# Attention 3 of a four-layer model: search for the largest scores in pairs and by chunks of keys, preparation in steps over more PSUM banks

## The chip, the cores and the metric

The kernel runs as one program on one core of a Trainium2 chip. The metric is the device time in microseconds (us), the median of several runs. Five engines matter: PE (TensorE, matrix products and transposes, which write to PSUM), DVE (VectorE), ACT (ScalarE), POOL (GpSimd) and the DMA queues, which have nothing to do in the stage that is edited. PSUM has eight banks; each bank here holds one tile of 512 float32 columns.

## The reference, cut to what matters

The input is an image pair `x` of shape (2, 56, 56, 128). Layers 0 and 1 are state-space blocks, layer 2 is an attention and a spectral mixer, layer 3 an attention and a layer of experts. The edited code belongs to the two attentions, above all the one of layer 3, over L = 3136 tokens of each of two images:

```python
def _L3_attn_ref(x, Wq, bq, Wk, bk, Wv, bv):
    TEMP = (2 * 128) ** 0.5
    q = jnp.einsum('bnf,of->bno', x, Wq) + bq
    k = jnp.einsum('bnf,of->bno', x, Wk) + bk
    v = jnp.einsum('bnf,of->bno', x, Wv) + bv
    scores = jnp.einsum('bnf,bmf->bnm', q, k) / TEMP
    alpha = jax.nn.softmax(scores, axis=-1)
    out = jnp.einsum('bnm,bmf->bnf', alpha, v)
    return out
...
t = _to_tokens(x)
t = t + _L2_attn_ref(_ln_t(t))
t = t + _L2_ffn_ref(_ln_t(t), L2_ffn_sigma, L2_ffn_phi, L2_ffn_M_u, L2_ffn_M_phi_plus, L2_ffn_M_phi_minus, L2_ffn_log_weights, L2_ffn_gumbel)
t = t + _L3_attn_ref(_ln_t(t), L3_attn_Wq, L3_attn_bq, L3_attn_Wk, L3_attn_bk, L3_attn_Wv, L3_attn_bv)
t = t + _L3_ffn_ref(_ln_t(t), L3_ffn_gate_w, L3_ffn_gate_b, L3_ffn_weight1, L3_ffn_weight2)
```

Layer 2's attention (`_L2_attn_ref`) is the same without projections: queries, keys and values are the normalised tokens, and a token doesn't attend to itself.

## The kernel before

The kernel does the layers one after the other. Layer 2's attention is `Attention2`, then comes the mixer, then layer 3's attention, `Attention3`, then the experts. Both attentions run the class `Attend`.

**Attend.run** goes over 14 chunks of queries: two images (`b`) with seven chunks (`qc`) of 448 tokens each. A chunk goes in 25 steps `j` over tiles of 128 keys (the last has 64). In a step PE makes the scores of the key tile against the 448 queries (L1031, into a bank `sc`), ACT takes the exponential into a tile `e` (L1033), POOL adds `e` to `total` (L1042, L1044), and PE adds the product of the values with `e` to the accumulator `acc`, in a bank `av` (L1025). This last product lags by two steps. At the end of the chunk DVE copies `acc` to `by` (L1055), PE multiplies it with the output weights (L1059, into `pt`) and sums `total` over keys with a column of ones (L1062, into `pd`, a second tile of the pool `av`), DVE takes the reciprocal (L1066) and adds the scaled result to the tokens `X` (L1069). A float32 product of 448 columns is two instructions in the trace.

**Queries** is for layer 3 alone. The exponential needs a shift, an estimate of the largest score of each query. `begin` makes the queries of a chunk (L949, bank `lo`), adds a bias on ACT (L953) and casts them to bfloat16 (L955). `some(left)` then works off a list of 28 search tiles: four groups `i` of 112 queries by seven chunks `c` of keys. Each is one bfloat16 product (L966, into the bank `lo`, of which there is one) and one maximum on DVE (L971). The list has `i` outside and `c` inside; after the seventh tile of a group, the maximum of the seven maxima is taken (L973) and turned into a row by PE (L974, into a bank `pr` that is held over the whole search). After the fourth group ACT copies the row (L980), PE spreads it over 128 partitions (L982) and DVE adds it to the queries (L983), which the scores of the chunk wait for. While a chunk is worked on, the next chunk's search is issued step by step, so that after step `j` at most `28 * (21 - j) // 21` tiles are left.

**Attention3.run** first prepares the seven chunks of image 0, with `chunk`: it adds the mixer's result `A`, turned by PE (L1180), to the tokens (L1181), normalises them (`layernorm_tokens`: L77 to L83 on DVE, with a square and a square root on ACT, L80 and L82, and a product on POOL, L84), turns them into channels (L1189), evacuates these to `uT`, casts a bfloat16 copy `low` on POOL (L1192) and turns key tiles into values (`key_tiles`, L1202). All banks of a chunk come from `sc`. The chunks of image 1 are prepared by the function `then`, at the end of the query chunks of image 0, with the bank `pt`: one at the end of each of the chunks 0 to 4, and two at the end of chunk 5.

PSUM in `Attend` is divided into three banks `sc`, two `av`, and one each of `lo`, `pr` and `pt`.

The order in which an engine gets its instructions is made by the framework when the program is built, from the order in the source, the dependencies and the buffers; in the trace the first query (L949) stands between the second and third preparation, although the source issues it after the seventh. At run time an engine follows its fixed order.

Of the kernel before, what the change touches and what calls it, by code (L numbers as in the profile page):

```python
# [14 lines left out]
F32 = mybir.dt.float32  # L15
BF16 = mybir.dt.bfloat16
# [103 lines left out]
class Scans:  # L120
# [177 lines left out]
    def run(self):  # L298
        with ExitStack() as ctx:
            self.open(ctx)  # L300
            with self.k.tc.manual_schedule():
                self.all_steps()
# [622 lines left out]
def four(ps):  # L925

    return ps[:TP].rearrange("p (i c) -> p i c", c=C)


class Queries:  # L930
# [13 lines left out]
    def begin(self, b, qc):  # L944
        nc = self.k.nc
        self.b = b
        self.todo = [(i, c) for i in range(4) for c in range(NCH)]
        ps = self.banks("lo")
        nc.tensor.matmul(  # L949
            ps[:, 0:CH], lhsT=self.weights, rhs=self.keys[b][:, CH * qc : CH * (qc + 1)], start=True, stop=True  # L950
        )
        self.q = self.sp.tile([128, CH], F32, name="q")
        nc.scalar.activation(self.q, ps[:, 0:CH], AF.Identity, bias=self.bias)  # L953
        self.q16 = self.sp.tile([128, CH], BF16, name="q16")
        nc.vector.tensor_copy(self.q16, self.q)  # L955
        self.rows = self.banks("pr")

    def some(self, left):

        nc = self.k.nc  # L960
        while len(self.todo) > left:
            i, c = self.todo.pop(0)
            if c == 0:
                self.m = self.sp.tile([TP, NCH + 1], F32, name="m")
            ps = self.banks("lo")[:TP, 0:CH]
            nc.tensor.matmul(  # L966
                ps, lhsT=self.q16[:, TP * i : TP * (i + 1)], rhs=self.low[self.b][:, CH * c : CH * (c + 1)],
                start=True, stop=True,
            )
            m = self.m  # L970
            nc.vector.tensor_reduce(m[:, c : c + 1], ps, AX.X, ALU.max)  # L971
            if c == NCH - 1:
                nc.vector.tensor_reduce(m[:, NCH : NCH + 1], m[:, 0:NCH], AX.X, ALU.max, negate=True)  # L973
                nc.tensor.matmul(  # L974
                    self.rows[0:1, TP * i : TP * (i + 1)], lhsT=m[:, NCH : NCH + 1],
                    rhs=self.k.ident[:TP, :TP], start=True, stop=True,
                )
                if i == 3:
                    row = self.sp.tile([1, CH], BF16, name="shift")
                    nc.scalar.copy(row, self.rows[0:1, 0:CH])  # L980
                    ps = self.banks("pr")[:, 0:CH]
                    nc.tensor.matmul(ps, lhsT=self.part, rhs=row, start=True, stop=True)  # L982
                    nc.vector.tensor_tensor(self.q, self.q, ps, ALU.add)  # L983

    def take(self):
        self.some(0)
# [3 lines left out]
class Attend:  # L990
# [6 lines left out]
    def __init__(self, k, ctx):  # L997
        self.k = k
        self.sp = ctx.enter_context(k.pool("att", 6))
        self.ep = ctx.enter_context(k.pool("atts", 2))  # L1000
        pools = {"sc": 3, "av": 2, "lo": 1, "pr": 1, "pt": 1}
        self.pools = {n: ctx.enter_context(k.pool("p" + n, m, psum=True)) for n, m in pools.items()}
        self.ones = self.ep.tile([KT, 1], F32, name="onecol")
        k.nc.gpsimd.memset(self.ones, 1.0)
# [1 line left out]
    def bank(self, name):  # L1006
        return bank(self.pools[name], name)

    def run(self, keys, queries, V, scale, out_w, skip=None, then=lambda b, qc: None):

        k, nc, X = self.k, self.k.nc, self.k.X
        made = isinstance(queries, Queries)
        chunks = [(b, qc) for b in range(B) for qc in range(NCH)]
        if made:
            queries.begin(*chunks[0])
        for at, (b, qc) in enumerate(chunks):
            if made:
                q = queries.take()
            else:
                q = queries[b][:, CH * qc : CH * (qc + 1)]  # L1020
            acc = self.bank("av")[:, 0:CH]
            total = self.ep.tile([KT, CH], F32, name="total")

            def weigh(j, n, e):
                nc.tensor.matmul(acc, lhsT=V[b][:n, j, :], rhs=e[:n], start=j == 0, stop=j == NKT - 1)  # L1025

            waiting, first = [], None
            for j in range(NKT):
                n = min(KT, L - KT * j)
                ps = self.bank("sc")[:, 0:CH]  # L1030
                nc.tensor.matmul(ps[:n], lhsT=keys[b][:, KT * j : KT * j + n], rhs=q, start=True, stop=True)  # L1031
                e = self.sp.tile([KT, CH], F32, name="e")
                nc.scalar.activation(e[:n], ps[:n], AF.Exp, scale=scale)  # L1033
                if skip is not None:
                    c0, c1 = max(KT * j, CH * qc), min(KT * j + n, CH * (qc + 1))
                    if c0 < c1:
                        own = e[:n, c0 - CH * qc : c1 - CH * qc]
                        nc.vector.tensor_tensor(own, own, skip[:n, c0 - KT * j : c1 - KT * j], ALU.mult)  # L1038
                if j == 0:
                    first = e  # L1040
                elif j == 1:
                    nc.gpsimd.tensor_tensor(total, first, e, ALU.add)  # L1042
                else:
                    nc.gpsimd.tensor_tensor(total[:n], total[:n], e[:n], ALU.add)  # L1044
                if made and at + 1 < len(chunks):
                    if j == 0:
                        queries.begin(*chunks[at + 1])
                    queries.some(max(0, 28 * (21 - j) // 21))
                waiting.append((j, n, e))
                if len(waiting) > 2:  # L1050
                    weigh(*waiting.pop(0))
            for one in waiting:
                weigh(*one)
            by = self.ep.tile([128, CH], F32, name="by")
            nc.vector.tensor_copy(by, acc)  # L1055
            pt = four(self.bank("pt"))
            pd = self.bank("av")
            for i in range(4):
                nc.tensor.matmul(  # L1059
                    pt[:, i, :], lhsT=by[:, TP * i : TP * (i + 1)], rhs=out_w, start=True, stop=True  # L1060
                )
                nc.tensor.matmul(  # L1062
                    pd[:TP, i : i + 1], lhsT=total[:, TP * i : TP * (i + 1)], rhs=self.ones, start=True, stop=True
                )
            r = self.ep.tile([TP, 4], F32, name="r")
            nc.vector.reciprocal(r, pd[:TP, 0:4])  # L1066
            for i in range(4):
                xo = X[:, 4 * qc + i, b, :]
                nc.vector.scalar_tensor_tensor(xo, pt[:, i, :], r[:, i : i + 1], xo, ALU.mult, ALU.add)  # L1069
            then(b, qc)  # L1070


class Attention2:
# [40 lines left out]
class Attention3:  # L1114
# [35 lines left out]
    def run(self, A):  # L1150

        k = self.k
        with ExitStack() as ctx:
            kp = ctx.enter_context(k.pool("a3"))
            self.uT = [kp.tile([128, L], F32, name=f"u{b}") for b in range(B)]
            self.low = [kp.tile([128, L], BF16, name=f"low{b}") for b in range(B)]
            self.V = [kp.tile([KT, NKT, C], F32, name=f"V{b}") for b in range(B)]
            self.sp = ctx.enter_context(k.pool("a3u", 2))
            att = Attend(k, ctx)
            for c in range(NCH):  # L1160
                self.chunk(att, A, 0, c, "sc")

            def then(b, qc):

                if b == 0:
                    for c in {5: (5, 6), 6: ()}.get(qc, (qc,)):
                        self.chunk(att, A, 1, c, "pt")

            queries = Queries(k, self.uT, self.low, self.weights, self.c, att.ep, att.bank)
            att.run(self.uT, queries, self.V, 1.0 / 16, self.Wv, then=then)  # L1170

    def chunk(self, att, A, b, c, name):


        k, nc = self.k, self.k.nc
        x = k.X[:, 4 * c : 4 * (c + 1), b, :]
        ps = four(att.bank(name))
        for i in range(4):
            t = TP * (4 * c + i)
            nc.tensor.transpose(ps[:, i, :], A[:, b, t : t + TP], k.ident)  # L1180
# [3 lines left out]
        st = self.sp.tile([TP, 2, 4], F32, name="st")  # L1184
        layernorm_tokens(k, U, x, sq, st, C)
        nc.gpsimd.tensor_tensor(x, x, self.bias.unsqueeze(1).to_broadcast([TP, 4, C]), ALU.add)
        pt = att.bank(name)[:, 0:CH]
        for i in range(4):
            nc.tensor.transpose(pt[:, TP * i : TP * (i + 1)], U[:, i, :], k.ident[:TP, :TP])  # L1189
        uT = self.uT[b]  # L1190
        k.evacuate(uT[:, CH * c : CH * (c + 1)], pt, more=True)
        nc.gpsimd.tensor_copy(self.low[b][:, CH * c : CH * (c + 1)], uT[:, CH * c : CH * (c + 1)])  # L1192
        key_tiles(k, att.bank(name), uT, self.V[b], c)


def key_tiles(k, ps, uT, V, c):
# [679 lines left out]
```

## Time and profile before

| | |
|---|---|
| Time before | 9507.8 us, median of 3 runs (9499.12 to 9516.37) |
| The profiled execution's own time | 9515.81 us |
| Its span | 9513.7 us |
| PE busy in the span | 8186.0 us (86%) |
| Mean granted PE clock | 0.941 |
| Attention 2's chunks | 6081 to 6641 us |
| Attention 3, from its first transposes to its last accumulator | 8438.3 to 9271.9 us |
| Experts | 9274 to 9513.7 us |

The distances between the `by` copies (L1055), which end the accumulation of a chunk, show the pace of the chunks. In Attention 2 all are 40.0 us apart. In Attention 3 the first scores start at 8538.6, the first copy at 8584.6, and the distances are 52.0, 52.1, 52.0, 52.1, 52.0, 53.6 (image 0), 60.6, 52.3, 53.4, 55.2, 52.0, 54.8 and 45.1 us (image 1; in the last chunk no search follows).

How to read the profile: times are in us from the start of the span. A line of the timeline has the start, the duration, engine, source line, operation, the tiles it writes and reads, their shapes and a count; in brackets stand the idle time of the engine before it and what ended it. `PEld` is the load of weights into PE, which can run beside a product. The granted clock is the share of full speed that PE was given.

### The profile page before, as it was taken

What the parts mean: (1) busy time and instruction counts of PE and PEld (TensorE: products, weight loads), DVE (VectorE), ACT (ScalarE), POOL (GpSimd) and SP (SyncE); (2) the same over time, 40 slices, a digit from 0 to 9 for tenths busy, and PEclk for the clock granted to TensorE, in tenths of its full rate; (3) what the DMA queues carried; (4) which work ended last, traced back from release to release, by engine and by line L of the source; (5) the groups of instructions that cost most, each with busy time, mean ns of one, the idle gap of its engine ahead of it and who ended that gap; (6) DMA issues with size and microseconds to landing.
All of it is one profiled execution on the core that took longest, in us unless ns stands there. A gap on an engine that the chain in (4) does not pass through costs nothing. (4 is left out here: it accounts for less than half of the span.)

```text
span 9513.7 us, 94170 instructions
## 1 busy us (share of the span) xinstructions
PE 8186.0 (86%) x28803; PEld 4810.7 (51%) x28803; DVE 7093.3 (75%) x7484; ACT 3823.2 (40%) x6517; POOL 6321.7 (66%) x4006
## 2 busy tenths in 40 slices
PE   7888888888888888888888888699799999979997
PEld 3444444444444434444444444454688888854445
DVE  8999998999987997997998898401566766654433
ACT  4555545555445555555555555233111111113321
POOL 5999987999986996996997899666111111115550
PEclk9999999999999998998999999799899999979998
DMA  5766664666655884884885787000333333300005
GB/s 158 221 220 214 212 193 149 221 222 214 213 175 133 220 214 122 222 215 120 221 218 155 191 218 202 6 1 4 97 106 95 109 97 102 102 14 1 1 4 153
DMA packets 800676, 1367.59 MB, mean 144 GB/s; under 512 B 125373, under 2 KB 434366, under 8 KB 800138
## 3 DMA queue, kind: packets, MB, share of 16 engines
q1 hardware_dynamic: 800170, 1361.57, 50.2%
q8 instruction: 228, 3.74, 0.2%
q14 instruction: 278, 2.28, 0.1%
HBM read 1320.14 MB, written 41.11 MB: 143 GB/s over the span
## 5 line engine op out<-in xcount | busy, mean ns | idle before, releaser
L423 POOL TENSOR_TENSOR p<-h,c 128x784 f32<-128x784 f32 x2048 | 3762.5, 1860 | 238.9 <-PE acc L371 159.0
L371 PE MATMUL acc<-p,ident 128*128 128x392 f32 x8192 | 3138.5, 514 | 87.6 <-POOL p L423 86.0
L351 DVE TENSOR_TENSOR_SCAN h<-a,state,h 128x784 f32<-128x784 f32 x1536 | 2798.2, 1841 | 92.3 <-ACT a L332 70.4
L371 PEld LDWEIGHTS acc<-p,ident 128*128 128x128 f32 x8192 | 1523.6, 198 | 1178.6 <-POOL p L423 199.4
L410 DVE TENSOR_TENSOR h<-du,b 128x784 f32<-128x784 f32 x1408 | 1335.7, 949 | 182.5 <-PE b L357 178.5
L332 ACT ACTIVATE a<-delta,L0A 128x784 f32<-128x784 f32 x1024 | 938.8, 918 | 838.2 <-DVE h L351 836.4
L426 POOL TENSOR_TENSOR h<-du,b 128x784 f32<-128x784 f32 x640 | 1188.2, 1857 | 3.1 <-DMA b<-rows 3.1
L357 PE MATMUL b<-three,sel 96*128 96x512 bf16 (+1 forms) x2816 | 711.0, 334 | 551.7 <-DVE h L410 502.7
L332 ACT ACTIVATE a<-delta,L1A 128x784 f32<-128x784 f32 x1024 | 936.5, 917 | 535.5 <-DVE h L351 533.3
L351 DVE TENSOR_TENSOR_SCAN h<-a,h 128x784 f32<-128x784 f32 x512 | 901.9, 1780 | 39.8 <-ACT a L332 21.4
L1044 POOL TENSOR_TENSOR total<-total,e 128x448 f32<-128x448 f32 (+1 forms) x644 | 727.5, 1130 | 293.6 <-ACT e L1033 266.4
L1425 POOL TENSOR_TENSOR u<-u,S 128x1024 f32<-128x1024 f32 x64 | 150.0, 2365 | 1136.5 <-DVE S L1394 1136.5
L1394 DVE TENSOR_TENSOR u<-u,cv 128x512 f32<-128x512 f32 x1024 | 623.4, 681 | 342.7 <-PE cv L1381 341.3
L357 PEld LDWEIGHTS <-sel 96*128 96x128 bf16 x2816 | 276.0, 98 | 1163.8 <-issue 920.3
L1033 ACT ACTIVATE e<-sc 128x448 f32<-128x448 f32 (+1 forms) x700 | 379.7, 543 | 775.2 <-PE sc L1031 748.4
L971 DVE TENSOR_REDUCE m<-lo 112x1 f32<-112x448 f32 x392 | 244.7, 624 | 371.3 <-PE lo L966 370.0
L1396 ACT COPY u<-cv 128x512 f32<-128x512 f32 x256 | 149.3, 586 | 850.9 <-PE cv L1381 776.6
L1566 PE MATMUL pj<-u,Wm 128*128 128x196 f32 (+8 forms) x1536 | 354.5, 384 | 5.7 <-DVE A L1572 5.7
L1031 PE MATMUL sc<-q,u 128*128 128x448 f32 (+1 forms) x700 | 334.2, 566 | 7.3 <-DVE q L983 7.3
L1031 PE MATMUL sc<-big 128*128 128x448 f32 (+1 forms) x700 | 322.3, 546 | 12.4 <-ACT e L1033 12.4
L385 PE MATMUL acc<-big,ident 128*128 128x392 f32 x384 | 250.5, 784 | 92.4 <-ACT big L391 92.3
L1025 PE MATMUL av<-e,big 128*128 128x448 f32 (+1 forms) x700 | 320.6, 545 | 1.2 <-DVE e L1038 1.2
(394 smaller groups left out, 10527.4 us busy)
## 6 DMA issues: line engine op xcount, KB each, us to landing
c<-rows SPq DMA_DIRECT2D x1024, 392.0 KB, 4.0
c<-rows SPq DMA_DIRECT2D x2048, 196.0 KB, 4.4
b<-rows SPq DMA_DIRECT2D x320, 392.0 KB, 4.6
b<-rows SPq DMA_DIRECT2D x640, 196.0 KB, 4.5
H<-raw SPq DMA_DIRECT2D x32, 1568.0 KB, 7.0
wC<-win SPq DMA_DIRECT2D x64, 576.0 KB, 5.7
wA<-win SPq DMA_DIRECT2D x64, 384.0 KB, 5.4
wD<-win SPq DMA_DIRECT2D x64, 320.0 KB, 4.4
```

The source lines that it names most:

```text
L332: self.k.nc.scalar.activation(x["a"], g["delta"][ci], AF.Exp, scale=self.w["A"](g["kd"], ci, x["n"]))
L351: self.k.nc.vector.tensor_tensor_scan(h, a, h, start, ALU.mult, ALU.add)
L357: self.k.nc.tensor.matmul(ps[:, c0:c1], lhsT=self.w["selB"](x["n"]), rhs=x["g"]["three"][:, c0:c1], start=True, stop=True)
L371: nc.tensor.matmul(job["acc"][:, i, 0:392], lhsT=self.k.ident, rhs=x["p"][:, 392 * i : 392 * (i + 1)], start=False, stop=n == NS - 1,)
L410: nc.vector.tensor_tensor(one["h"], one["g"]["du"][one["ci"]], one["b"], ALU.mult)
L423: nc.gpsimd.tensor_tensor(now["p"], now["h"], now["c"], ALU.mult)
L426: nc.gpsimd.tensor_tensor(three["h"], three["g"]["du"][three["ci"]], three["b"], ALU.mult)
L1031: nc.tensor.matmul(ps[:n], lhsT=keys[b][:, KT * j : KT * j + n], rhs=q, start=True, stop=True)
L1033: nc.scalar.activation(e[:n], ps[:n], AF.Exp, scale=scale)
L1044: nc.gpsimd.tensor_tensor(total[:n], total[:n], e[:n], ALU.add)
L1394: nc.vector.tensor_tensor(place(o), place(o), ps, ALU.add)
L1566: nc.tensor.matmul(ps[:, lo - c0 : hi - c0], lhsT=Ws[f][:, eo, r, :], rhs=u[:, b, f, lo - a0 : hi - a0], start=f == 0, stop=f == 1,)
```

## The change

The diff touches both classes and the preparation:

- The list of search tiles has the chunks of keys outside and the groups of queries inside. The maxima of all tiles are kept in one tile `m`; when the list is empty one instruction takes the maximum of the seven for all four groups, and the four turns into a row follow one another.
- `lo` has two banks, `pt` is gone. The output product uses `pr`, and the row and its spread take banks `pr` only at the end of the search. `pd` becomes four columns of the bank of `acc`.
- In the chunks, after step `j` at most `30 - 2j` tiles are left.
- In the preparation `chunk` is split into `tokens`, `channels` and the existing `key_tiles`. For image 0, the tokens of the next chunk are issued ahead of the channels of this one, with banks `av` for the tokens and `sc` for the rest; the first query is made after the first chunk's channels, and four search tiles follow each chunk.
- Image 1 is prepared within the query chunks 0 to 3, two chunks in each of the first three and one in the fourth, by `also`, which is called in every step: tokens in step 1, channels in step 6, key tiles in step 9, and the same twelve steps later. All use the bank `pr`.

```diff
-        self.todo = [(i, c) for i in range(4) for c in range(NCH)]
+        self.todo = [(c, i) for c in range(NCH) for i in range(4)]
...
-        self.rows = self.banks("pr")
+        self.m = self.sp.tile([TP, 4, NCH], F32, name="m")
...
+            nc.vector.tensor_reduce(self.m[:, i, c : c + 1], ps, AX.X, ALU.max)
+        if not self.todo:
+            m = self.sp.tile([TP, 4], F32, name="mm")
+            nc.vector.tensor_reduce(m, self.m, AX.X, ALU.max, negate=True)
+            ps = self.banks("pr")
+            for i in range(4):
                 nc.tensor.matmul(
-                    self.rows[0:1, TP * i : TP * (i + 1)], lhsT=m[:, NCH : NCH + 1],
-                    rhs=self.k.ident[:TP, :TP], start=True, stop=True,
+                    ps[0:1, TP * i : TP * (i + 1)], lhsT=m[:, i : i + 1], rhs=self.k.ident[:TP, :TP],
+                    start=True, stop=True,
                 )
...
-        pools = {"sc": 3, "av": 2, "lo": 1, "pr": 1, "pt": 1}
+        pools = {"sc": 3, "av": 2, "lo": 2, "pr": 1}
...
-                    queries.some(max(0, 28 * (21 - j) // 21))
+                    queries.some(max(0, 30 - 2 * j))
                 waiting.append((j, n, e))
                 if len(waiting) > 2:
                     weigh(*waiting.pop(0))
+                also(at, j)
...
-            pt = four(self.bank("pt"))
-            pd = self.bank("av")
+            pt = four(self.bank("pr"))
+            pd = av[:TP, CH : CH + 4]
...
-            then(b, qc)
...
-                self.chunk(att, A, 0, c, "sc")
-
-            def then(b, qc):
-
-                if b == 0:
-                    for c in {5: (5, 6), 6: ()}.get(qc, (qc,)):
-                        self.chunk(att, A, 1, c, "pt")
...
+            U = {0: self.tokens(att.bank("av"), A, 0, 0)}
             for c in range(NCH):
+                if c + 1 < NCH:
+                    U[c + 1] = self.tokens(att.bank("av"), A, 0, c + 1)
+                self.channels(att.bank("sc"), U.pop(c), 0, c)
+                if c == 0:
+                    queries.begin(0, 0)
+                key_tiles(k, att.bank("sc"), self.uT[0], self.V[0], c)
+                queries.some(4 * (NCH - 1 - c))
+
+            def also(at, j):
+
+                half, part = divmod(j, 12)
+                c = 2 * at + half
+                if half > 1 or c >= NCH:
+                    return
+                if part == 1:
+                    U[c] = self.tokens(att.bank("pr"), A, 1, c)
+                elif part == 6:
+                    self.channels(att.bank("pr"), U.pop(c), 1, c)
+                elif part == 9:
+                    key_tiles(k, att.bank("pr"), self.uT[1], self.V[1], c)
+
+            att.run(self.uT, queries, self.V, 1.0 / 16, self.Wv, also=also)
```

`tokens` is the first half of `chunk` up to the bias on the tokens, and `channels` the second half up to the bfloat16 copy; their instructions are unchanged.

## The prediction

> **What bounds the kernel now.** I read the page first (TensorE, PE, busy 86% of the span), then the sums over windows for the stages that the edited code runs in, then the timeline inside them. The page's chain of waits was no help: it ends in the experts after this stage. The windows, from Attention 2 to the end (columns: stretch, length, busy time and count of PE, weight loads, DVE, ACT, POOL, then granted PE clock, DMA share, GB/s):
>
> ```profile
> 6081.00:6641.00 560.00, 558.03 (x1608) 281.52 (x1608) 43.10 (x135) 191.68 (x354) 380.16 (x342) 1.00 0.01 3
> 8438.30:8506.00 67.70, 23.85 (x95) 16.75 (x95) 29.95 (x59) 10.31 (x21) 20.01 (x21) 0.56 0.00 0
> 8506.00:8538.60 32.60, 17.32 (x38) 5.09 (x35) 16.03 (x30) 2.80 (x4) 0.00 (x0) 0.50 0.00 0
> 8538.60:8898.40 359.80, 346.58 (x1136) 176.44 (x1135) 161.93 (x312) 128.17 (x223) 208.74 (x189) 0.99 0.00 1
> 8898.40:9271.90 373.50, 353.68 (x1059) 174.77 (x1060) 134.47 (x260) 101.74 (x188) 189.79 (x168) 0.94 0.00 1
> ```
>
> Attention 2 (first row) runs its 14 chunks in 40.0 us each with PE always busy: the price of a chunk without search. Attention 3 has three parts: preparation of image 0 (67.7 us, no engine busy for half of it, PE clock 0.56), the rest of the first search (32.6 us), and the chunks, 733.3 us for 14, so 52.4 each. What is late in the second part is one bank, seen in the timeline:
>
> ```profile
> 8518.09 0.62 DVE L971 TENSOR_REDUCE m<-lo 112x1 f32<-112x448 f32 x1 [0.62 <-PE lo L966]
> 8518.76 0.53 PE L966 MATMUL lo<-low,q 128*112 128x448 bf16 x1 [0.71 <-DVE m L971]
> 8518.77 0.17 PEld L966 LDWEIGHTS <-q 128*112 128x112 bf16 x1 [1.07 <-issue]
> 8519.33 0.62 DVE L971 TENSOR_REDUCE m<-lo 112x1 f32<-112x448 f32 x1 [0.62 <-PE lo L966]
> 8520.01 0.53 PE L966 MATMUL lo<-low,q 128*112 128x448 bf16 x1 [0.71 <-DVE m L971]
> ```
>
> PE and DVE take turns: one tile of the search every 1.25 us, of which DVE works 0.62. The same happens between chunks, where the rest of the search stands before the next chunk's scores:
>
> ```profile
> 9121.80 0.38 PE L1059 MATMUL pt<-L3Wv,by 128*112 128x128 f32 x2
> 9122.68 1.02 PE L949 MATMUL lo<-u,M 128*128 128x448 f32 x2 [0.50 <-DVE m L971]
> 9123.63 0.35 PE L974 MATMUL pr<-ident,m 112*1 112x112 f32 x2
> 9124.83 0.34 PE L982 MATMUL pr<-shift,part 1*128 1x448 bf16 x1 [0.84 <-ACT shift L980]
> 9126.24 3.32 PE L1031 MATMUL sc<-q,u 128*128 128x448 f32 x4 [1.06 <-DVE q L983]
> ```
>
> From 9121.8 to 9126.2 PE has about 1.5 us of work; the rest is waiting for the chain maximum, transpose, copy, spread, add. And the preparation is one chain per chunk of tokens:
>
> ```profile
> 8454.81 1.01 PE L1189 MATMUL sc<-ident,U 112*128 112x112 f32 x4 [3.45 <-POOL U L84]
> 8456.53 1.11 PE L1202 MATMUL sc<-ident,u 128*128 128x128 f32 x4 [0.72 <-DVE u L62]
> 8457.44 1.06 PE L1180 MATMUL sc<-ident,A 128*112 128x128 f32 x4
> 8458.29 0.58 PE L966 MATMUL lo<-low,q 128*112 128x448 bf16 x1
> 8464.59 1.01 PE L1189 MATMUL sc<-ident,U 112*128 112x112 f32 x4 [5.71 <-POOL U L84]
> ```
>
> L1189 to L1189 is 9.8 us; the next chunk's first transposes (L1180) start only behind L1202, so two chains hardly overlap.
>
> **What the Trainium skill says.** TensorE: Matmul & The Clock Gate, Part 1 (What's actually happening): an array that has been idle runs at half clock, and some 3.4 us of sustained work release it. The trace agrees: granted clock 0.50 in the lone search, 1.00 in Attention 2, 0.94 for image 1's chunks. Trace Analysis (Optimizing Tensor Performance, Matmuls) advises rotating independent groups through PSUM banks so that evacuation overlaps the next group; the 1.25 us rhythm shows the want of it. PSUM — Partial Sum Buffer (PSUM bank collisions raise a hardware error): a bank must not be written by PE while DVE reads another part of it. No run here shows it, but it bears on an edit below: the denominators `pd` move into the bank that the copy `by` reads, so they should wait for that copy.
>
> **The change part by part.**
>
> *Preparation of image 0.* The same instructions in another order: tokens of c+1 stand before channels of c, in other banks, and four search tiles follow each chunk (chunk-outer order needs only the keys of that chunk). The chain from L1180 to the end of L84 is 7.1 us (8457.44 to 8464.54), and with two in flight it no longer sets the pace. DVE then does: per chunk 0.69+0.68+0.17+0.69+0.69+0.18 for the normalisation and 0.62 for the evacuation, 3.7 us, times 7 is 26.0; 28 reductions of 0.625 are 17.5; the cast of q 0.4. That is 44 us in 78 instructions; with about 0.06 us between two of them, 49. Ahead of DVE lie 0.8 us of transposes, about 4 us of idle DVE while only the first chains run, and behind it the chain to the first scores: after the last reduction before it took 4.9 us (8533.7 to 8538.6), 2.4 of which were the next query's L949; I take 4, and 4 for unlucky order. Sum 62 instead of 100.3: **gain 38** (28 if the pace is 8.3 us a chunk, 45 if DVE has no gaps). The table of ACT isn't concerned: no Exp runs there yet.
>
> *Search inside the chunks, two banks, two tiles a step.* What PE must do in a chunk: 40.0 (Attention 2's row), 28 search tiles at 0.19 (step between their starts in the loop) 5.3, L949 0.95, four L974 at 0.28 1.1, L982 0.2: 47.55. Preparing one chunk of image 1 adds 3 x 0.45 = 1.35 us. Chunks 1 to 5 do all this today in 52.0, so 48.9 is work and 3.1 waiting; image 1's chunks take 52.0 to 60.6 (54.8 in the mean) for 47.55 of work, because nothing is there to fill the waits and the clock falls to half for 3.4 to 13.7 us each time. With the budget 30-2j the last tile is issued at step 15 of 25, so the chain to q has nine steps (some 17 us) and ends before the chunk does; then the next scores can follow without a gap, as in Attention 2. Two tiles in a step cost DVE 2 x 0.625 plus gaps, 1.35 us, in a step of 1.5+0.38 = 1.88 us of PE: it fits, with 0.5 us to spare.
> The `by` copy is 0.62 us; the eight L1062 that ran beside it must now wait, and the next scores fill the place (three `sc` banks). Cost nothing; without that cover 0.7 x 28 = 20 us over both attentions.
> After, chunk by chunk, from first scores to the last `by`: chunk 0 46.0 + 2.7 (two preparations) + 2.6 (three more tiles and the chain) = 51.3; chunks 1 and 2 50.25; chunk 3 48.9; chunks 4 to 12 9 x 47.55 = 428; chunk 13 40.3. Sum 669, against 733: 64.
>
> *Image 1's preparation in three steps inside chunks 0 to 3.* Its PE work is in the sum. Its Sqrt takes ACT from the Exp table and back: 2 x 1.28 us of table loads, seven times before and after (ScalarE: Activation LUTs, What ACT_TABLE_LOAD costs, gives the same 1283 ns), so ACT is away for some 3.5 us while weighting lags scores by two steps (3.4 us). Its DVE operations (3.7 us) come into steps where the search uses 1.35 of 1.88. From the three steps of PE, the second stands 5 steps (9.4 us) behind the first; that chain took 8.9 us in chunk 2 before (8640.5 to 8649.4) and stalled PE 0.48. POOL has 27.1 us of sums in a chunk, plus 5.7 for two preparations: room enough. I charge 1 us for each of seven: 7 (between 0 and 21). **Gain of the chunks 57** (between 43 and 64).
>
> *Attention 2* uses the same class: its `pt` becomes `pr`, one bank as before, and `pd` as above: 0. The experts behind start earlier and are unchanged.
>
> Sum: 38 + 57 = 95 us of the profiled execution's 9515.8 (span 9513.7), which gives 9421. The median shown is 9507.8, 8 lower, within the 17 us by which its runs differ; against it the forecast is **9413**.
>
> **The rivals.**
> - *The loop keeps its waits* (9460). PE follows a fixed order, and if reductions and normalisation crowd DVE in chunks 0 to 3, or the chain to q is ordered late, the loop gains only some 10 us and preparation 38. For it: 0.5 us of slack in a step against DVE operations of 0.69. Against: in chunks 4 to 12 DVE has nothing else.
> - *More than that* (9385): preparation at 6 us a chunk (7 more) and an interior free of stalls (7), and PE warm before the first scores, with the chain to q hidden in part (14). For it: the clock gate's price is in all of today's gaps.
> - *Slower: the pair holds PE* (9606). If the second tile of a pair, in the fixed order, has to wait until the first is reduced, as with one bank, each step grows from 1.88 to 1.5+0.19+1.25 = 2.94 us: 1.06 us in 14 steps of 13 chunks, 193 us, less the 95. It decides from 0.52 us a pair (95 / 182). For it: DVE's in-order queue, busy 72% in these steps. Against: two banks free one after the other, and the second reduction ends about 1.7 us after the pair began, before its bank is wanted again at 2.07.
> - *Nothing happens* (9500): the order on the engines is made by the framework, which already pulled the first query's L949 ahead of the second chunk's end; it might undo the written order. Against: the banks, which bound it, do change.
>
> **How the numbers follow.** Likeliest 0.70 (its own range 9385 to 9440, from the bounds 28 to 45 and 43 to 64), loop keeps its waits 0.13, more 0.05, slower 0.08, nothing 0.04. The range 9378 to 9470 leaves out the last two and some tails. A measurement here tells 0.2% (19 us) from no change: faster 0.86, same 0.05, slower 0.09.
>
> **What would show it.** Right: first scores about 62 us after the first L1180; `by` copies 47.5 apart for chunks 4 to 12 with clock 1.00; no DVE wait ahead of the first scores of a chunk. Wrong: search matmuls in the loop that wait for `m` by 0.5 us or more; L1189 waiting for U by several us; `by` copies of Attention 2 no longer 40.0 apart.

## The result, and the profile after

The median went from 9509.49 us to **9401.65 us** (four runs each, 9499.12 to 9516.37 and 9399.84 to 9417.94): ratio 0.9891, 95% interval 0.9874 to 0.9908. The prediction knew three of the four runs before, with a median of 9507.8; its forecast was 9413 us with a range of 9378 to 9470. The profiled execution took 9399.84 us, span 9398.0.

The same sums over windows, of the changed kernel; the columns are those of the first view of the prediction. The rows are image 0's preparation, chunk 2 of the queries, chunks 4 to 12 together, and the last chunk:

```profile
8424.00:8482.00 58.00, 38.64 (x132) 20.91 (x131) 42.92 (x87) 12.65 (x25) 20.88 (x21) 0.56 0.00 1
...
8582.00:8634.10 52.10, 50.51 (x179) 26.73 (x179) 26.87 (x51) 22.92 (x37) 32.89 (x30) 1.00 0.00 0
...
8684.50:9112.70 428.20, 428.20 (x1396) 222.66 (x1396) 177.77 (x337) 132.87 (x243) 244.51 (x216) 1.00 0.00 1
9112.70:9152.70 40.00, 40.00 (x117) 20.16 (x116) 1.93 (x6) 13.61 (x25) 27.18 (x24) 1.00 0.00 1
```

From chunk 4 on PE is busy for 428.20 of 428.20 us at full clock: nine chunks at 47.6 us. The preparation with the first search, 100.3 us before, takes 57.9. The clock there is still 0.56; in a second profile of the changed kernel it was 0.62, for the same 57.9 us: that difference of the clock didn't change the length of the stage.

The seam between two chunks, in the timeline of PE (before, the seam shown in the prediction had waits of 0.50, 0.84 and 1.06 us):

```profile
8683.46 1.02 PE L1025 MATMUL av<-e,V 64*128 64x448 f32 x2
8684.41 1.02 PE L1031 MATMUL sc<-q,u 128*128 128x448 f32 x2
8685.26 0.92 PE L949 MATMUL lo<-u,M 128*128 128x448 f32 x2
8686.01 0.38 PE L1060 MATMUL pr<-L3Wv,by 128*112 128x128 f32 x2
8686.23 0.27 PE L1063 MATMUL av<-onecol,total 128*112 128x1 f32 x2
...
8687.60 1.75 PE L1031 MATMUL sc<-q,u 128*128 128x448 f32 x4
8689.19 0.54 PE L966 MATMUL lo<-low,q 128*112 128x448 bf16 x2
8689.57 0.92 PE L1025 MATMUL av<-e,V 128*128 128x448 f32 x2
```

No line has a bracket, so PE waits for nothing. The next chunk's first scores (L1031) and the next query (L949) stand directly behind the last accumulation, and the denominators (L1063) come after them, when the copy `by` has read the bank. Search tiles come in pairs (`x2`).

Where the time went, from one stage to the next (us; each row is read from the two traces):

| stage | before | after | difference |
|---|---|---|---|
| start to Attention 2's first `by` copy | 6120.9 | 6109.7 | -11.2 |
| to Attention 3's first transposes | 2317.4 | 2314.4 | -3.0 |
| first transposes to first scores | 100.3 | 57.9 | -42.4 |
| first scores to last `by` copy | 733.3 | 670.7 | -62.6 |
| rest, the experts above all | 241.8 | 245.3 | +3.5 |

The edited stage gives 105.0 us of the 115.7 between the two spans, and the medians differ by 107.8. The first row is, up to one chunk of Attention 2, code that the change doesn't touch; over all traces of changed versions it spread from 6105.4 to 6123.0, and the changed kernel itself, run again, had 6114.9 there and 2317.5 in the second row. So neither row can be told from drift between executions. The last row was 244.0 to 245.8 in all changed versions but one; why it is longer than before was not looked into. Read stages, not spans, to judge parts of 5 us.

### The profile page after: what moved, and what is told of

It is laid out like the page before. It is cut to its first block, busy times and chain, and to the rows that moved or that the text cites. A ratio compares the mean times of both kernels' runs of the same rounds, so it can differ in the third digit from the quotient of the medians.

```text
span 9398.0 us, 94099 instructions
## 1 busy us (share of the span) xinstructions
PE 8136.1 (87%) x28803; PEld 4794.3 (51%) x28803; DVE 7072.4 (75%) x7442; ACT 3832.5 (41%) x6517; POOL 6320.6 (67%) x4006
## 5 line engine op out<-in xcount | busy, mean ns | idle before, releaser
L371 PE MATMUL acc<-p,ident 128*128 128x392 f32 x8192 | 3127.5, 513 | 87.4 <-POOL p L423 85.8
L1044 POOL TENSOR_TENSOR total<-total,e 128x448 f32<-128x448 f32 (+1 forms) x644 | 729.9, 1133 | 322.3 <-ACT e L1033 294.5
L1031 PE MATMUL sc<-big 128*128 128x448 f32 (+1 forms) x700 | 323.8, 548 | 12.5 <-ACT e L1033 12.5
L1031 PE MATMUL sc<-q,u 128*128 128x448 f32 (+1 forms) x700 | 323.0, 546 | 0.2 <-DVE q L984 0.2
```

The costliest lines, as they stand in the source:

```text
L371: nc.tensor.matmul(job["acc"][:, i, 0:392], lhsT=self.k.ident, rhs=x["p"][:, 392 * i : 392 * (i + 1)], start=False, stop=n == NS - 1,)
```

## The experiments

Every run below is judged by two lengths in its own trace: preparation (first transposes to first scores; 100.3 before, 57.9 after) and chunks (first scores to last `by` copy; 733.3 and 670.7). Both repeat closely: the changed kernel, run again, had 57.9 and 670.7. Edits are against the changed kernel.

### One bank for the search

```diff
-        pools = {"sc": 3, "av": 2, "lo": 2, "pr": 1}
+        pools = {"sc": 3, "av": 2, "lo": 1, "pr": 1}
```

> The changed kernel with one bank lo again (the eighth bank stays empty), all else kept, the pace of two search tiles a step too. Theory of the prediction (the bank lets two tiles go in a step): with one bank each second tile waits for the first one's reduction; if PE stands still for it, chunks 4 to 12 grow from 47.6 to 47.6 + 14 x 1.06 = 62 us. Rival (the order on the engines is made around the bank: the tiles are spread one to a step over the whole chunk as in the kernel before, and the second bank is worth only the tail): chunks 4 to 12 between 49 and 53 us. Rival (the bank is worth nothing, the list by chunks and the early end of the search are): 47.6 us. Preparation from first transposes to first scores: 58 us if DVE sets it, 62 to 68 if PE has to take turns with DVE there.

Preparation 62.1, chunks 740.5; chunks 7 to 12 took 54.5 to 54.6 us each. The whole gain of the chunks is gone, and 7.2 us more. The timeline of PE inside a chunk and behind it:

```profile
8838.42 0.35 PE L966 MATMUL lo<-low,q 128*112 128x448 bf16 x1
8838.61 0.92 PE L1025 MATMUL av<-e,V 128*128 128x448 f32 x2
8839.36 0.92 PE L1031 MATMUL sc<-q,u 128*128 128x448 f32 x2
8840.11 0.35 PE L966 MATMUL lo<-low,q 128*112 128x448 bf16 x1
8840.30 0.92 PE L1025 MATMUL av<-e,V 128*128 128x448 f32 x2
```
```profile
8851.14 0.53 PE L966 MATMUL lo<-low,q 128*112 128x448 bf16 x1 [0.71 <-DVE m L970]
8851.71 0.62 DVE L970 TENSOR_REDUCE m<-lo 112x1 f32<-112x448 f32 x1 [0.62 <-PE lo L966]
8852.37 0.18 DVE L973 TENSOR_REDUCE mm<-m 112x4 f32<-112x28 f32 x1
8852.39 1.86 PE L949 MATMUL lo<-u,M 128*128 128x448 f32 x2 [0.72 <-DVE m L970]
8854.18 1.65 PE L976 MATMUL pr<-ident,mm 112*1 112x112 f32 x8
...
8857.68 2.05 PE L1060 MATMUL pr<-L3Wv,by 128*112 128x128 f32 x8
8859.52 3.31 PE L1031 MATMUL sc<-q,u 128*128 128x448 f32 x6
```

Inside the chunk nothing waits: there is one search tile a step, though the source asks for two, because the order was made around the bank. The price stands at the seam. The search isn't done when the chunk ends, so the chain to the next queries runs with little beside it: 11.0 us from the `by` copy at 8848.5 to the next scores at 8859.5. The clock falls to half with it, for 10.2 us from 8851.1, and again at each of the seams that follow. That is the rival's mechanism, and more than its 53 us. The sums over all chunks, of this kernel and of the changed one, show how the price is made up:

```profile
8484.90:9225.40 740.50, 715.88 (x2192) 367.73 (x2192) 295.21 (x532) 232.39 (x412) 399.28 (x357) 0.93 0.00 1
8482.00:9152.70 670.70, 665.93 (x2191) 346.71 (x2191) 280.48 (x532) 233.69 (x412) 400.22 (x357) 1.00 0.00 1
```

PE waits for 24.6 us with one bank and for 4.8 with two, 20 us more. With one bank it also works for 99 us at half clock, which at full clock would have been half as long: 49 us, an estimate. Together they make up the 69.8 us between the two, and the larger part is the clock's.

### One bank, old pace

```diff
-        pools = {"sc": 3, "av": 2, "lo": 2, "pr": 1}
+        pools = {"sc": 3, "av": 2, "lo": 1, "pr": 1}
...
-                    queries.some(max(0, 30 - 2 * j))
+                    queries.some(max(0, 28 * (21 - j) // 21))
```

> The changed kernel with one bank lo and the old pace, so that of the search only the order of the list and the combined end are new. In the run with one bank and the new pace the chunks took 54.5 us. Theory (the bank sets it): chunks 4 to 12 between 50 and 54.5 us, since one tile fits a step and the rest of the search stands at the end of the chunk as in the kernel before. Rival (with one bank it was the pace of two tiles a step that hurt, and the old pace is free of it): below 49 us.

Preparation 62.1, chunks 717.9; chunks 4 to 12 from 49.1 to 54.8. The clock stayed whole up to chunk 4: chunks 0 to 4 took 48.9 to 50.4, four of them with preparations of image 1, and chunks 5 to 12, with falls of 3.4 to 10.2 us, took 51.3 to 54.8. With one bank the pace of two a step costs 22.6 us (740.5 - 717.9); by the same estimate 19 of them are the clock's (61 us of work at half clock instead of 99) and 4 are waits. Everything else that is new in the chunks (order of the list, combined end, `pr` in place of `pt`, bank of the denominators, image 1's place) is worth 733.3 - 717.9 = 15.4 us.

### Two banks, old pace

```diff
-                    queries.some(max(0, 30 - 2 * j))
+                    queries.some(max(0, 28 * (21 - j) // 21))
```

> The changed kernel with two banks lo but the old pace of the search (at most 28 * (21 - j) // 21 tiles left after step j, so the last is issued in step 21 instead of 15). Theory (the bank is what was missing, the pace follows from it): chunks 4 to 12 at 47.6 us, total as the changed kernel. Rival (the end of the search in step 15 is needed to hide the chain from the largest scores to the next queries, 4 to 5 us): with four steps of 1.7 us left behind the search the chain is late by a little and each chunk grows by 1 to 3 us, 13 to 39 us in all.

Preparation 57.9, chunks 666.3. Chunks 4 to 12 stay at 47.6, and chunks 1 to 3, which carry image 1's preparation, go from 52.2, 52.2 and 50.4 to 50.7, 50.7 and 49.5. So the faster pace isn't needed to hide the chain to the next queries, and costs 4.4 us where the search meets the preparation: PE's waits for a search bank in chunks 0 to 3 (L966 for `m`), 2.7 us in the changed kernel, are gone here. Against the run with one bank and the same pace, the second bank alone gives 717.9 - 666.3 = 51.6 us in the chunks.

### Old order of image 0's preparation

```diff
-                if c + 1 < NCH:
-                    U[c + 1] = self.tokens(att.bank("av"), A, 0, c + 1)
-                self.channels(att.bank("sc"), U.pop(c), 0, c)
-                if c == 0:
-                    queries.begin(0, 0)
+                u = self.tokens(att.bank("sc"), A, 0, c)
+                self.channels(att.bank("sc"), u, 0, c)
                 key_tiles(k, att.bank("sc"), self.uT[0], self.V[0], c)
-                queries.some(4 * (NCH - 1 - c))
+            queries.begin(0, 0)
```

> The changed kernel with image 0 prepared in the old order (tokens, channels and key tiles of one chunk, all from the banks sc, then the next chunk; the first search issued after all), list by chunks of keys and two lo banks kept. If tokens issued ahead in banks of their own are what shortens preparation (theory): first transposes to first scores stays at 68 us for the seven chunks plus up to 18 us of search (28 tiles at 0.65) and 5 us of chain, 75 to 91 us. Rival (the list by chunks does it, since the framework lifts search tiles into the gaps anyway): 73 us or less, and most of the 42 us that were gained stay. The chunks stay at 47.6 us.

Preparation 80.4, chunks 672.2. Timeline of PE:

```profile
8462.95 0.53 PE L966 MATMUL lo<-low,q 128*112 128x448 bf16 x1 [0.59 <-DVE m L970]
8467.41 1.01 PE L1204 MATMUL sc<-ident,U 112*128 112x112 f32 x4 [3.92 <-POOL U L84]
8469.22 1.08 PE L1215 MATMUL sc<-ident,u 128*128 128x128 f32 x4 [0.81 <-DVE u L62]
8470.10 1.06 PE L1190 MATMUL sc<-ident,A 128*112 128x128 f32 x4
8470.96 0.95 PE L966 MATMUL lo<-low,q 128*112 128x448 bf16 x2
```

The next chunk's transposes (here L1190) are behind this chunk's key tiles again, and the channels (L1204) wait for the normalised tokens. Four search tiles follow each chunk although the source issues them after all seven: the framework lifts them. So the early place in the source isn't what brings the search beside the preparation. Tokens ahead in banks of their own, with the early search, give 22.5 us; a later pair of runs leaves the search out of the difference (29.2 us). The order of the tokens and their banks were changed together in every run, so which of the two does it is not shown.

### The same with one bank, and the same with the old list

The old order once with `"lo": 1`, and once with the list `[(c, i) for i in range(4) for c in range(NCH)]`.

> The changed kernel with the old order of the preparation and one bank lo, list by chunks of keys. The kernel before took 100.3 us from first transposes to first scores, the old order with list by chunks and two banks 80.4. If the list by chunks gave those 20 us (the search goes along with the preparation): 80 to 85 us here. If the second bank gave them (a tile of the rest in 0.65 us instead of 1.25): 95 to 101 us.

Preparation 81.1, chunks 735.2: the price of one bank in the chunks again.

> The changed kernel with the old order of the preparation and the list by groups of queries, two banks lo. If the list by chunks gave the 20 us with the old order: 21 tiles stand behind the preparation, at 0.65 us, and 5 us of chain, 68 + 14 + 5 = 85 to 90 us from first transposes to first scores. If the bank gave them all: 80 us.

Preparation 87.4, chunks 672.2. With the old order, the list by chunks is worth 7.0 us with two banks, and makes the second bank worth next to nothing (0.7).

### New order, list by queries

```diff
-        self.todo = [(c, i) for c in range(NCH) for i in range(4)]
+        self.todo = [(c, i) for i in range(4) for c in range(NCH)]
...
-                if c == 0:
-                    queries.begin(0, 0)
                 key_tiles(k, att.bank("sc"), self.uT[0], self.V[0], c)
-                queries.some(4 * (NCH - 1 - c))
+            queries.begin(0, 0)
```

> The changed kernel with the old order of the list (groups of queries outside, chunks of keys inside), so that the first search can't follow the preparation; tokens issued ahead in banks av kept. Theory (two gains add up: overlapped chains, and the search beside them): preparation of seven chunks in 40 to 50 us, then 21 tiles of search at 0.65 us, 14 us, and 5 us of chain: 59 to 69 us from first transposes to first scores. Rival (the overlap alone gives it all, DVE being the bound either way): 58 us. Rival (the overlap is worth nothing without the search beside it): over 85 us. Inside the chunks the order of the list shouldn't matter: 47.6 us.

Preparation 58.2, chunks 670.7: nothing lost. Against the old order with the same list, whose search is issued late too, only the tokens ahead and their banks differ: 87.4 - 58.2 = 29.2 us. The last channels are evacuated 36.2 us after the mixer's last addition instead of 47.0, and 22 of the first query's tiles follow alone, one every 0.63 us. So the two gains don't add up, and the first rival's 58 us came. Either the search lies beside the preparation and slows it, or it follows at two banks' speed. The cases side by side, in us (the kernel before differs in the other edits too):

| preparation | list by queries | list by chunks |
|---|---|---|
| old order, one bank | 100.3 (before) | 81.1 |
| old order, two banks | 87.4 | 80.4 |
| new order, one bank | not run | 62.1 |
| new order, two banks | 58.2 | 57.9 (after) |

### Image 1 at the end of the chunks

```diff
+                if j < NKT - 1 or at >= NCH:
+                    return
+                for c in {5: (5, 6), 6: ()}.get(at, (at,)):
+                    u = self.tokens(att.bank("pr"), A, 1, c)
+                    self.channels(att.bank("pr"), u, 1, c)
+                    key_tiles(k, att.bank("pr"), self.uT[1], self.V[1], c)
```

in place of the body of `also`.

> The changed kernel with image 1 prepared where it was before: at the end of query chunks 0 to 5 (two at the end of 5), all in the one bank pr, all else kept. Theory (the place doesn't matter much, since in all cases a preparation has 1.35 us of PE work and stalls of about 1 us): chunks 1 to 6 near 49 to 50 us, total within 5 us of the changed kernel. Rival (steps within the chunk are needed, since a chain at the end of the chunk holds the bank pr and with it the output and the next shift): chunks 1 to 6 at 51 to 53 us, total 10 to 25 us longer.

Preparation 57.9, chunks 670.0: chunk 0 takes 45.1 instead of 47.8, chunks 1 to 6 take 49.6 to 51.1, the sum is within 1 us of the changed kernel's. At the new pace of the search, where image 1 is prepared is worth next to nothing.

### A bank of its own for the denominators

```diff
-            pd = av[:TP, CH : CH + 4]
+            pd = self.bank("av")[:TP, 0:4]
```

> The changed kernel with the four columns of denominators in a bank of the pool av of their own, as before the change, instead of the bank that is copied to by. Theory (the products L1063 have to wait for the copy, and the next scores cover it): Attention 2 at 40.0 us a chunk and chunks 4 to 12 at 47.6 us in both. Rival (the wait costs 0.7 us a chunk): 39.3 and 46.9 us. Rival (a tile of av of its own takes the bank that the next accumulator wants, and costs up to 1 us).

Preparation 57.8, chunks 668.4, chunks 4 to 12 at 47.6 to 47.9, Attention 2 at 40.0. The wait for the copy costs nothing there, as the seam above shows. Chunks 1 to 3 are 2.8 us shorter (51.2, 51.2, 49.5), and two later ones 0.3 us longer. PE's waits in chunks 0 to 3 fall from 4.8 to 2.7 us: those for POOL's normalised tokens (L1207 for `U`), 2.1 us in the changed kernel, are gone. What in the order removes them was not looked into.

### Less on DVE, and the best of the parts

Image 1 at the end of the chunks, and two operations off DVE: image 0's channels are evacuated by ACT, and the mean is scaled by `tensor_tensor` with a tile of 1/128.

```diff
-    nc.vector.tensor_scalar_mul(mean, mean, 1.0 / d)
+    nc.vector.tensor_tensor(mean, mean, over, ALU.mult)
...
-        k.evacuate(self.uT[b][:, cs], ps[:, 0:CH], more=True)
+        nc.scalar.activation(self.uT[b][:, cs], ps[:, 0:CH], AF.Identity, bias=k.one)
```

> Image 1 prepared at the end of the chunks (as in that run), and two operations taken off DVE: image 0's channels are evacuated by ACT, and the mean is scaled by a product of two tensors instead of a product with a constant, which in the changed kernel's trace ended together with POOL's operation when one ran beside it (0.67 to 1.05 us instead of 0.16). Theory (DVE sets the pace of the preparation): 7 x 0.62 + 2 x 0.8 = 6 us off the 58 us from first transposes to first scores, and up to 0.7 us off each of chunks 0 to 6; total 6 to 10 us below 9396.5. Rival (the order and the latencies of the chain set it, since DVE is busy 43 of 58 us): within 2 us of 58.

Preparation 55.2, chunks 670.1; 9403.36 us (9396.72 to 9423.58), ratio to before 0.9895 (0.9878 to 0.9911). DVE's busy time in the preparation fell from 42.9 to 39.1 us, not by the 6 expected (the scaling of the mean still took 0.80 us where POOL worked beside it, as the last section shows), and the preparation by 2.7: DVE sets a part of its pace, but isn't all of it. In the chunks nothing was gained.

> What the runs so far favour, together: two banks lo, new order in the preparation of image 0 with less on DVE, image 1 at the end of the chunks, and the old pace of the search. If the parts add up: 55 us from first transposes to first scores, chunks in 664 to 668 us, and about 5 to 8 us less than the changed kernel from the mixer's end to the last accumulator. In the medians against the kernel before this can't be told from the changed kernel, ratio 0.988 to 0.990.

Preparation 56.2, chunks 671.8; 9416.36 us (9412.56 to 9425.16), ratio 0.9905 (0.989 to 0.9919). The parts don't add up: with image 1 at the end of the chunks, the old pace gives nothing (chunks 1 to 5 at 49.6 to 49.7 with either pace). With image 1 in steps and the old pace, the run above had the shortest chunks of all, 666.3. And the trace has 256.5 us behind the last `by` copy instead of 245. First this kernel, then the changed one again, timeline of PE in the experts:

```profile
9241.50 22.29 PE L1688 MATMUL pp<-selT,U 112*128 112x64 f32 x104
```
```profile
9243.69 1.00 PE L1686 MATMUL pp<-selT,U 112*128 112x64 f32 x8
9244.97 11.05 PE L1686 MATMUL pp<-selT,U 112*128 112x64 f32 x98
```

The same series of small products, in code that no edit touches, runs at half clock in the first and at full clock in the second.

> The changed kernel once more, on the same chip as the last run. Preparation 58 us and chunks 671 us again if these are fixed by the order on the engines; the time up to Attention 2's first copy may differ by some 10 us from execution to execution, as it did between the profiles of before and after (6120.9 and 6109.7), if that is drift of the layers ahead and not the change.

9409.86 us (9402.24 to 9423.33), ratio 0.9899 (0.9883 to 0.9916). No version beat the changed kernel by more than these intervals.

## Why the prediction was right

- **What the chunks cost.** "What PE must do in a chunk" was summed to 47.55 us; chunks 4 to 12 took 47.58. The last chunk was put at 40.3 and took 40.0. This is the term that carries the forecast, and it came from one row of Attention 2 and the steps between starts on PE. That it is right to 0.03 us is luck: in chunk 4 the added instructions take 7.20 us from start to start (28 tiles 5.30, L949 0.75, L976 0.86, L983 0.29) where 7.55 were put, and the rest takes 40.38, not 40.0. Each half is right to 0.4 us.
- **What was late.** The prediction held that one bank leaves a rest of the search at the seams, and that the clock falls there. The runs with one bank show it. Its reading of the seam was off, though: the lines from 9121.8 to 9126.2 add up to 2.0 us of work, not 1.5, beside 2.4 us of waits. The second bank is worth 51.6 us at the old pace and 69.8 at the new.
- **Chunks 0 to 3.** Forecast 51.3, 50.25, 50.25 and 48.9, with 1 us more for each of seven preparations; measured 47.8, 52.2, 52.2 and 50.4. The charge was right for chunks 1 to 3 (5.3 us against 5). Chunk 0 was over-sized by 5.5 us. Its base of 46.0 us held no waits (PE was busy throughout), but a clock at half until 8542.3, worth 1.85 us, which went; little of the 2.6 us for more tiles and the chain came, since three tiles of the next search stand ahead of the first scores; and PE waited 0.5 us there, not 2. Sum 669 before the charge, 670.7 measured; with the charge the forecast gained 57 and the chip 62.6. The waits that remain, on PE and on DVE in chunk 1:

```profile
8539.50 0.35 PE L966 MATMUL lo<-low,q 128*112 128x448 bf16 x1 [0.45 <-DVE m L970]
...
8545.05 0.60 PE L1207 MATMUL pr<-ident,U 112*128 112x112 f32 x4 [0.69 <-POOL U L84]
```
```profile
8537.34 0.61 DVE L970 TENSOR_REDUCE m<-lo 112x1 f32<-112x448 f32 x1
8537.87 1.05 DVE L78 TENSOR_SCALAR st<-st 112x4 f32<-112x4 f32 x1
```

- **Preparation.** Forecast 62, measured 57.9: shorter by as much as was put for unlucky order. DVE worked 42.9 us where 44 were put. The reason given was half right. Overlapping the chains does what was said (22.5 us with the list by chunks, 29.2 without). But the list by chunks, to which the prediction gave the hiding of the search, isn't needed once the chains overlap (58.2 without it), and DVE, 42.9 us busy of 58, isn't the only pace-maker: of 3.8 us taken off it 2.7 arrived.
- **The budget of 30-2j** was said to let the chain to the queries end early and so make the seam smooth. The seam is smooth at the old pace too, with two banks and not with one: the bank does it.
- **Image 1 in steps** was charged, not credited; the run with it at the end of the chunks has the same sum within 1 us, so at this pace it is worth next to nothing.
- **The denominators** were costed at nothing with the next scores as cover; the seam shows that cover.
- **The slower rival**, that the second tile of a pair holds PE, didn't occur with two banks: in chunks 4 to 12 PE never waits. With one bank too it took another form, since the order on PE is made with the bank known, and tiles are spread, not held.
- **The whole.** In the stage 95 us were forecast and 105.0 came: 4.4 more in the preparation and 5.6 more in the chunks, nearly all in chunk 0. These are two of the terms of the rival "more than that", the faster preparation and PE warm before the first scores. The 9385 given as the lower end of the likeliest case does not follow from its bounds: 45 + 64 = 109 us lead to 9399.

## What to carry to other kernels

To price a stage that is bound by one engine, look for the same loop elsewhere in the program without the suspected waits: its period plus the added work gave the chunk to 0.1 us here, with two errors of 0.4 us that cancelled. A short chain that ends behind a loop costs more than its length when PE's clock falls with it (of the 69.8 us above, about 49 by the estimate), and a bank that lets its work go beside the loop removes both. Where the framework orders the instructions, buffers decide and the place in the source often doesn't: of six edits two, the second bank and the tokens ahead in their own banks, carried most of the gain. The pace of the search is the exception: it is set in the source alone, and cost 22.6 us with one bank and 4.4 with two.

## What the runs showed of the hardware that was not expected

A DVE operation on four elements a partition can wait for a whole operation of POOL. In the changed kernel the scaling of the mean (L78, `tensor_scalar`) took 0.16 to 0.17 us when POOL was idle, and 0.67 to 1.05 us in chunks 0 to 3, each time ending within 0.03 us of the end of POOL's addition (L1044) that ran beside it. PE then waited 0.45 us for a search bank after six of the seven, 2.7 us in all. The line of POOL that belongs to the 1.05 us of L78 at 8537.87, shown above:

```profile
8537.76 1.13 POOL L1044 TENSOR_TENSOR total<-total,e 128x448 f32<-128x448 f32 x1 [0.79 <-ACT e L1033]
```

The Trainium skill, SBUF — State Buffer (Who interferes with whom), says that such a DVE operation and POOL can contend for a pair of ports that one of them holds for its whole instruction; the trace agrees. It says the same of a DVE product of two tensors in SBUF beside a POOL operation that reads SBUF, and the run with less on DVE agrees: as `tensor_tensor` the scaling took 0.15 to 0.16 us in its preparation and chunks where POOL was idle, and 0.80 us in the one place where an operation of POOL ran on beside it:

```profile
8457.26 1.04 POOL L87 TENSOR_TENSOR U<-U,st 112x512 f32<-112x512 f32 x1 [1.93 <-DVE st L86]
8457.52 0.80 DVE L81 TENSOR_TENSOR st<-st,over 112x4 f32<-112x4 f32 x1
```

So the other instruction doesn't avoid the wait. In the chunks of that run POOL was idle at those times, because image 1 is prepared at the end of the chunks, and with the old instruction in the same place it took 0.16 to 0.17 us as well; what the wait costs in the chunks is not shown by it.

PE's clock fell to half without any long pause. In the kernel with one bank it fell for 10.2 us at each of the later seams, where the longest single wait shown for PE is 0.72 us; in the last 3.4 us before the fall at 8851.1 PE was busy for 2.3. In the preparation it stood at 0.56 in the mean with PE busy 38.64 of 58.0 us. The Trainium skill, TensorE: Matmul & The Clock Gate (Part 1, What's actually happening), says that the clock follows how busy PE has been recently, and names an idle window of some 3.4 us for the slow state. The trace shows that no pause of that length is needed: a run of short waits was enough.

In the experts the same series of products ran at either clock from one kernel to the next, for a difference of some 10 us. In the slow case PE was busy for 22.29 of 22.30 us and the clock stayed at half throughout, so there the 3.4 us of sustained work that the prediction took from the same page didn't release it. What decides in that series stays open.
